# Three groups of transposes and an earlier-planned carry in a 16-batch attention-and-mixing block

## The chip, the cores and the metric

The kernel runs on one core of a Trainium2 chip. The metric is the device time of one execution in microseconds; the median of several runs is compared. A profile is one further execution, with a record of every instruction of the five engines: PE (matrix products; its weight loads are shown as PEld), DVE (vector), ACT (scalar), POOL (general purpose) and SP, which here only issues DMA transfers.

## What is computed

The input x has 16 batches of 512 rows and 512 columns, ctx 16 batches of 512 rows and 1024 columns. Per batch, cut to what matters:

```python
h  = layernorm(x)                                  # rows
h  = rmsnorm(h, g_res) @ W_in.T + b_in             # "a" product
u  = rmsnorm(ctx, g_init)[:, :512] * const
s  = scan(s[t] = a * s[t-1] + u[t])                # over the 512 rows
x1 = x + h + s[plug]                               # gather of rows
y  = layernorm(x1);  yp = y shifted down by one row
k  = square(relu((mu_k*y + (1-mu_k)*yp) @ W_k.T))  # "k" product
r  = sigmoid((mu_r*y + (1-mu_r)*yp) @ W_r.T)       # "r" product
out = x1 + r * (k @ W_v.T)                         # "v" product
```

The rows plug come from running sums of an integer mask.

## The kernel before

**Tiling.** A batch's 512 rows lie on 128 partitions, four rows to each (j = 0 to 3). Each product of 512 x 512 by 512 x 512 is made of four output tiles of 128 x 512, and each tile of three passes of four matmuls: both operands are split into a high part that was rounded to fp32r and the rest, and high by high, high by low and low by high are added (`QW`, `gemm` at line 880). A tile's sum stands in one PSUM slot of the pool "ps". There are four such slots (`SLOTS`, line 308), and four of "tr" for transposes. In the trace the tiles are called pa, pk, pr and pw for the a, k, r and v products, their operands xh (x), m (mixed y) and ka (k after its square), each with the weights wh and wl.

**The chain of one batch.** ctx comes into cx tiles (five slots, four used by a batch). ACT squares them with a row sum (`sq`, line 707), POOL takes the power, DVE scales cx and runs the scan over the four rows of a partition (`scan_u`). What is carried from partition to partition is one more product, the carry pc (`scan`, line 744; from batch 2 on `carry3`, three matmuls of the high and low parts ch and cl). DVE adds pc to the four cx tiles, and SP writes them to a scratch tensor dr in DRAM (`put`, line 775). x comes in by a DMA; its statistics (`stat1`, line 654) go before b_in is added by a DMA that accumulates (`add_b`, line 696). Rows of dr are then gathered into x by four indirect DMAs on POOL that add (`gather`, line 816); from batch 4 on they come ahead of the a product's end (`NLATE`, line 438). `a_end` (line 809) is the DVE operation that adds pa, scaled, to x and so frees the PSUM slot. `norm2` (line 823) takes the statistics of x1 on DVE and makes y on ACT. `transp` (line 848) turns y, four 128 x 128 transposes on PE for each j, into the four tr tiles, and `mix` (line 860) makes m of them for k and for r: ACT writes pv, DVE adds to it, ACT rounds to the high part, and DVE or POOL takes the low part. Behind a k product ACT applies relu and the square and rounds (`k_mm`, line 904); behind r, ACT the sigmoid (sg); behind v, DVE multiplies by sg and DVE or POOL adds to x, which SP stores.

**What sets the order.** Every such step is a piece, given to a planner by `add`. The first loop over batches gives each PE piece a due time (lines 1078 to 1090): in period i come the a product of batch i+1, the k product of batch i, and then the tiles r0, r1, v0, r2, v1, r3, v2, v3 of batch i, numbered k = 0 to 7. `TAT` and, for named periods, `TAT_OF` (lines 320 and 321) say behind which k which transposes j of batch i+1 stand. `deadlines` (line 90) computes each piece's latest start backward from what needs it, where the piece's own length (`span`, line 58) includes its lead, and once more from the number of slots: who needs a slot that a later piece takes must be done before that. `order` (line 119) then runs through the engines and takes for each the ready piece with the earliest latest start, if its slots are free; it hands out the lowest free slot number. The program is written in this order, and each engine works its queue in that order, waiting at an instruction whose inputs or slot are not ready. SP's loads also wait for the PE piece that the plan has some time ahead of them (line 1272).

So a changed lead or due time can move any piece on any engine, and which slot a tile is given.

```python
lead=LEAD if b > 1 else 0.0          # of the carry, lines 750 and 767; LEAD = 12.0, line 441
return self.lead + s + (...)         # span, line 60
for jj in TAT_OF.get(i, TAT).get(k, ()):
    slot(("t", i + 1, jj), 0.43)     # lines 1087 and 1088
```

Of the kernel before, what the change touches and what calls it, by code (L numbers as in the profile page):

```python
# [316 lines left out]
}  # L317
PASS = 0.935
PERIOD = lambda i: (("a", i + 1), ("k", i))
TAT = {0: (0, 1), 2: (2, 3)}  # L320
TAT_OF = {0: {0: (0, 1, 2, 3)}, 1: {0: (0, 1, 2, 3)}, 2: {0: (0, 1, 2, 3)}}
AHEAD = 20.0
EASE = 1.0
SKIP = 6.0
# [114 lines left out]
NWHOLE = 2  # L439
Y_DVE = (0, 1, 2, 3)  # L440
LEAD = 12.0
HI_DVE = False
U_DVE = True
LOADS = ["raw2"]
# [7 lines left out]
def block_kernel(  # L452
# [59 lines left out]
    def add(engines, fn, r=(), w=(), new=None, **kw):  # L512
        if isinstance(engines[0], str):
            engines = (engines,)
        kinds = {}
        for n, v in (new or {}).items():
            kinds[n], spec[n] = v[0], v[1:]
        kw["stage"] = stage
        if engines is LO and ONLY.get(stage) is not None:
            kw["port"] = (DVE, POOL)  # L520
            engines = (LO[ONLY[stage]],)
        elif engines is HI:
            kw["port"] = (DVE,) if HI_DVE else ()
        elif engines is LO:
            kw["port"] = (DVE, POOL)
        elif engines[0][0] == POOL and "moves" not in kw:
            kw["port"] = (POOL,)
        plan.add(engines, fn, r, w, kinds, **kw)

    def K(name, *parts):  # L530
        return [(name, p) for p in (parts or (0,))]
# [4 lines left out]
    PS = (("ps",), [P, D], F32)  # L536
    PST = (("ps", "tr"), [P, D], F32)
    TRP = (("tr", "ps"), [P, D], F32)
    TR = (("tr",), [P, D], F32)
    HI = ((ACT, 0.52), (DVE, 0.34)) if HI_DVE else ((ACT, 0.52),)  # L540
    LO = ((DVE, 0.61), (POOL, 1.26))
# [202 lines left out]
    def scan(b):  # L744
        def carry(e):
            e.matmul(S[f"pc{b}"], scan_m, S[f"cx{b}_{NJ - 1}"][:, :D], start=True, stop=True)

        if b < NWHOLE:
            add((PE, 1.12), carry, K(f"cx{b}_{NJ - 1}") + K("consts"), K(f"pc{b}"),
                new={f"pc{b}": PST if b == 0 else PS}, lead=LEAD if b > 1 else 0.0)  # L750
        else:
            last, hi, lo = f"cx{b}_{NJ - 1}", f"ch{b}", f"cl{b}"
            TMPR = (("tmp",), [P, D], F32R)
            if b == NWHOLE:
                add((ACT, 0.3), lambda e: e.copy(scan_hi, scan_m), K("consts"), K("scan_r", 0))
                add((DVE, 0.2), lambda e: e.tensor_tensor(scan_lo, scan_m, scan_hi.bitcast(F32), ALU.subtract),
                    K("consts") + K("scan_r", 0), K("scan_r", 1))
            add((ACT, 0.52), lambda e: e.copy(S[hi], S[last][:, :D]), K(last), K(hi), new={hi: TMPR})
            add(LO, lambda e: e.tensor_tensor(S[lo], S[last][:, :D], S[hi].bitcast(F32), ALU.subtract),
                K(last) + K(hi), K(lo), new={lo: TMPR})  # L760

            def carry3(e):
                for i, (w, m) in enumerate(((0, hi), (0, lo), (1, hi))):
                    e.matmul(S[f"pc{b}"], (scan_hi, scan_lo)[w], S[m], start=(i == 0), stop=(i == 2))

            add((PE, 0.72), carry3, K(hi) + K(lo) + K("scan_r", 0, 1), K(f"pc{b}"),
                new={f"pc{b}": PS}, lead=LEAD if b > 1 else 0.0)
        for j in J:
            n = f"cx{b}_{j}"
            add((DVE, 0.6),  # L770
                lambda e, n=n, j=j: e.scalar_tensor_tensor(
                    S[n][:, :D], S[f"pc{b}"], ADEC ** (j + 1), S[n][:, :D], ALU.mult, ALU.add),
                K(f"pc{b}"), K(n))

            def put(e, n=n, j=j):
                if f"dr{b}" not in S:
                    S[f"dr{b}"] = dpool.tile([T, D], F32, tag="dr", name=f"dr{b}")
                e.dma_start(S[f"dr{b}"].rearrange("(p j) d -> p j d", j=NJ)[:, j], S[n][:, :D])

            add((SP, 0.5), put, K(n), K(f"dr{b}", j), moves=0.73)  # L780
# [288 lines left out]
    def slot(key, cost=3 * PASS):  # L1069
        nonlocal t  # L1070
        due[key] = t
        t += cost
# [5 lines left out]
    for i in range(NB):  # L1078
# [5 lines left out]
        for k, (w, j) in enumerate((("r", 0), ("r", 1), ("v", 0), ("r", 2), ("v", 1), ("r", 3), ("v", 2), ("v", 3))):  # L1084
            slot((w, i, j))
            if n1:
                for jj in TAT_OF.get(i, TAT).get(k, ()):
                    slot(("t", i + 1, jj), 0.43)
# [62 lines left out]
    def prepare_batch(b):  # L1151
# [34 lines left out]
        for j in J:  # L1186
            scan_u(b, j, one_go=b == 0 or U_DVE)
        scan(b)
        stage = ("stat1", b)
        for j in J:  # L1190
# [141 lines left out]
```

## Time and profile before

| | |
|---|---|
| median of 3 runs | 815.05 us (812.93 to 817.34) |
| profiled execution | 813.32 us, of which 811.2 us is the span from first to last instruction |
| granted clock of PE in it | 0.997 |
| matmul of a pass, 128 x 512, mean of a row | 396 to 400 ns; starts 0.233 us apart |
| DVE, a_end (x from pa) | 744 ns |
| DVE, carry added to cx | 684 ns |
| ACT, relu of pk / square of cx | 596 / 1061 ns |
| POOL, issue of one gather | 1715 ns |
| gathers waited for on the chain that ended last | 5.8% of the span |

PE's matmuls overlap: a row says 0.4 us, but the next one starts 0.233 us after it, so four of them, one pass, take 0.933 us. Engine time is best read from the distance of two starts. A stage of one batch is found on PE's list by its first pr matmul. Where a line ends in brackets, the engine was idle for the time in them, and the name in them is what ended the idle time.

### The profile page before, as it was taken

What the parts mean: (1) busy time and instruction counts of PE and PEld (TensorE: products, weight loads), DVE (VectorE), ACT (ScalarE), POOL (GpSimd) and SP (SyncE); (2) the same over time, 40 slices, a digit from 0 to 9 for tenths busy, and PEclk for the clock granted to TensorE, in tenths of its full rate; (3) what the DMA queues carried; (4) which work ended last, traced back from release to release, by engine and by line L of the source; (5) the groups of instructions that cost most, each with busy time, mean ns of one, the idle gap of its engine ahead of it and who ended that gap; (6) DMA issues with size and microseconds to landing.
All of it is one profiled execution on the core that took longest, in us unless ns stands there. A gap on an engine that the chain in (4) does not pass through costs nothing.

```text
span 811.2 us, 11218 instructions
## 1 busy us (share of the span) xinstructions
PE 789.8 (97%) x3627; PEld 624.8 (77%) x3627; DVE 616.2 (76%) x1323; ACT 486.7 (60%) x950; POOL 449.8 (55%) x374
## 2 busy tenths in 40 slices
PE   7998999999999999999999999999999999999997
PEld 4776777877777887878787887888778787888885
DVE  6899799989789497686968779685876869784622
ACT  5937496555484566757455775646666564655640
POOL 2843676464675465763647566565665647571300
PEclk9999999999999999999999999999999999999999
DMA  9857486884784773847668392866559477350001
GB/s 321 271 96 263 101 235 175 280 216 131 157 232 131 181 232 74 241 166 198 156 140 242 74 268 107 218 198 184 135 130 246 136 173 216 66 141 2 27 27 52
DMA packets 52554, 134.69 MB, mean 166 GB/s; under 512 B 4752, under 2 KB 5264, under 8 KB 50576
## 3 DMA queue, kind: packets, MB, share of 16 engines
q1 hardware_dynamic: 35744, 102.39, 36.9%
q0 software_dynamic: 16608, 31.46, 23.0%
q8 instruction: 28, 0.46, 0.2%
q14 instruction: 30, 0.25, 0.1%
q10 hardware_dynamic: 144, 0.13, 0.0%
HBM read 85.73 MB, written 33.55 MB: 147 GB/s over the span
## 4 chain that ended last, share of the span: by engine, by line
PE 62%; DVE 12%; DMA 9%; POOL 6%; issue 5%; ACT 4%; SPq 0%; POOLq 0%; DVEq 0%; ACTq 0%
PE pk L300 19%; PE pr L300 15%; PE pw L300 14%; PE pa L300 11%; DMA x<-dr,plug 6%; DVE cx L300 4%; PE tr L300 3%; DVE pv L300 2%; DVE x L300 2%; POOL m L300 2%; DMA dr<-cx 2%; POOL x L300 2%; ACT pv L300 2%; PE pc L300 1%; ACT junk L300 1%
## 5 line engine op out<-in xcount | busy, mean ns | idle before, releaser
L300 POOL TENSOR_TENSOR m<-pv,m 128x512 fp32r<-128x512 f32 x79 | 117.1, 1492 | 54.6 <-ACT m L300 23.3
L300 PE MATMUL pr<-whr,m 128*128 128x512 f32 x512 | 141.7, 400 | 0.8 <-ACT sg L300 0.8
L300 PE MATMUL pa<-wha,xh 128*128 128x512 f32 x512 | 136.0, 400 | 5.6 <-DVE x L300 2.7
L300 POOL DMA_INDIRECT x<-dr,plug x64 | 109.8, 1715 | 55.8 <-DMA dr<-cx 16.8
L300 PE MATMUL pw<-whv,ka 128*128 128x512 f32 x512 | 138.9, 397 | 0.6 <-ACT sg L300 0.6
L300 PE MATMUL pk<-m,whk 128*128 128x512 f32 x512 | 134.4, 397 | 2.5 <-DVE x L300 2.1
L300 ACT ACTIVATE pv<-tr,om 128x384 f32<-128x384 f32 (+1 forms) x256 | 100.5, 488 | 57.7 <-PE tr L300 44.6
L300 PEld LDWEIGHTS pa<-wha,xh 128*128 128x128 f32 x512 | 94.8, 188 | 33.4 <-DVE x L300 7.3
L300 PEld LDWEIGHTS pk<-m,whk 128*128 128x128 f32 x512 | 95.2, 188 | 27.9 <-DVE x L300 2.9
L300 PEld LDWEIGHTS pw<-whv,ka 128*128 128x128 f32 x512 | 95.6, 188 | 24.1 <-ACT sg L300 1.8
L300 PEld LDWEIGHTS pr<-whr,m 128*128 128x128 f32 x512 | 94.0, 188 | 22.3 <-ACT sg L300 1.2
L300 DVE SCALAR_TENSOR_TENSOR pv<-tr,small,pv 128x511 f32<-128x511 f32 x128 | 95.0, 743 | 11.3 <-ACT pv L300 9.2
L300 ACT ACTIVATE y<-x,r 128x512 f32<-128x512 f32 x48 | 39.0, 816 | 97.3 <-DVE r L300 95.3
L300 DVE TENSOR_TENSOR sg<-pw,sg 128x512 f32<-128x512 f32 (+1 forms) x65 | 44.0, 678 | 55.6 <-PE pw L300 55.4
L300 POOL TENSOR_TENSOR xh<-raw,xh 128x512 fp32r<-128x512 f32 x48 | 64.4, 1348 | 39.1 <-ACT xh L300 22.6
L300 POOL TENSOR_TENSOR x<-x,sg 128x512 f32<-128x512 f32 x14 | 19.3, 1378 | 113.9 <-DVE sg L300 94.5
L300 ACT CAST m<-pv 128x512 fp32r<-128x512 f32 x128 | 73.2, 628 | 15.1 <-DVE pv L300 12.2
L300 ACT ACTIVATE junk<-cx 128x1024 bf16<-128x1024 f32 x64 | 67.9, 1061 | 12.3 <-DMA cx<-cx 11.6
L300 ACT ACTIVATE sg<-pr 128x512 f32<-128x512 f32 x64 | 38.1, 598 | 56.5 <-PE pr L300 47.3
L300 PE MATMUL pa<-wla,xh 128*128 128x512 f32 x256 | 70.4, 398 | 0.3 <-POOL wla L300 0.3
L300 PE MATMUL pw<-wlv,ka 128*128 128x512 f32 x256 | 70.7, 398 | 0.0
L300 PE MATMUL pr<-wlr,m 128*128 128x512 f32 x256 | 70.3, 396 | 0.0
(116 smaller groups left out, 1300.7 us busy)
## 6 DMA issues: line engine op xcount, KB each, us to landing
cx<-cx SPq DMA_DIRECT2D x64, 512.0 KB, 6.2
dr<-cx SPq DMA_DIRECT2D x64, 256.0 KB, 3.4
out<-x SPq DMA_DIRECT2D x31, 512.0 KB, 2.8
x<-x SPq DMA_DIRECT2D x15, 1024.0 KB, 4.9
x<-bc POOLq DMA_DIRECT2D x14, 1024.0 KB, 8.1
raw<-xT SPq DMA_DIRECT2D x26, 512.0 KB, 7.5
wsa<-winT SPq DMA_DIRECT2D x2, 512.0 KB, 4.4
x<-x SPq DMA_DIRECT2D x4, 256.0 KB, 7.0
```

Of the source, the lines that this page charges most:

```text
L300: r = self._tc.keep_in_program_order(op(*args, **kwargs))
```

## The change

In the general table the sixteen transposes of the next batch no longer stand in two groups of eight, behind r0 and v0, but in three: those of j = 0 behind r0 (four), j = 1 and 2 behind r1 (eight) and j = 3 behind r2 (four). Periods 3 and 4 are put into the table of exceptions with the groups they had, so the new grouping holds from period 5 on, which is the seventh batch's transposes (batch 6, counted from 0). The lead of the carry's piece is 15 instead of 12 from batch 6 on.

```diff
-TAT = {0: (0, 1), 2: (2, 3)}
-TAT_OF = {0: {0: (0, 1, 2, 3)}, 1: {0: (0, 1, 2, 3)}, 2: {0: (0, 1, 2, 3)}}
+TAT = {0: (0,), 1: (1, 2), 3: (3,)}
+TAT_OF = {0: {0: (0, 1, 2, 3)}, 1: {0: (0, 1, 2, 3)}, 2: {0: (0, 1, 2, 3)}, 3: {0: (0, 1), 2: (2, 3)}, 4: {0: (0, 1), 2: (2, 3)}}
...
 LEAD = 12.0
+LEAD_LATE = 15.0
+NLEAD = 6
...
             add((PE, 1.12), carry, K(f"cx{b}_{NJ - 1}") + K("consts"), K(f"pc{b}"),
-                new={f"pc{b}": PST if b == 0 else PS}, lead=LEAD if b > 1 else 0.0)
+                new={f"pc{b}": PST if b == 0 else PS}, lead=(LEAD if b < NLEAD else LEAD_LATE) if b > 1 else 0.0)
...
             add((PE, 0.72), carry3, K(hi) + K(lo) + K("scan_r", 0, 1), K(f"pc{b}"),
-                new={f"pc{b}": PS}, lead=LEAD if b > 1 else 0.0)
+                new={f"pc{b}": PS}, lead=(LEAD if b < NLEAD else LEAD_LATE) if b > 1 else 0.0)
```

No instruction is added or removed. In the order that the planner makes of it, PE's queue of one later period changes like this (batch numbers from 0, T for four transposes of one j, C for a carry, three passes to a product):

```
before   pa9_0  pa9_1  pa9_2  pa9_3   pk8_0 to pk8_3
         pr8_0  T9_0 T9_1  pr8_1 (C10 behind its first pass)  pw8_0  T9_2 T9_3  pr8_2  pw8_1  pr8_3  pw8_2  pw8_3
after    pa9_0  pa9_1 (C10 behind its first pass)  pa9_2  pa9_3   pk8_0 to pk8_3
         pr8_0  T9_0  pr8_1  T9_1 T9_2  pw8_0  pr8_2  T9_3  pw8_1  pr8_3  pw8_2  pw8_3
```

The queues of DVE, ACT, POOL and SP move with it: the four gathers of a batch, for instance, stand together in POOL's queue of the new kernel, where they stood between the low parts of m.

## The prediction

> **What bounds the kernel now.** I read the busy shares first, then PE's waits, then PE in order of time, then one 48 us period on every engine. PE leads by far.
>
> ```profile
> PE 789.8 (97%) x3627; PEld 624.8 (77%) x3627; DVE 616.2 (76%) x1323; ACT 486.7 (60%) x950; POOL 449.8 (55%) x374
> ```
>
> PE does the same products in every batch, so a batch has a floor, and what a batch takes above it is waiting. The stages below run from one batch's first receptance product (pr) to the next one's.
>
> ```profile
> 460.00:508.40 48.40, 48.05 (x213) 38.16 (x212) 37.82 (x76) 29.97 (x57) 30.11 (x25) 1.00 0.62 174
> 556.70:605.30 48.60, 47.63 (x226) 38.00 (x226) 36.62 (x84) 30.55 (x57) 28.66 (x24) 1.00 0.58 153
> 653.00:701.30 48.30, 47.97 (x212) 37.95 (x211) 37.91 (x76) 29.99 (x57) 30.07 (x25) 1.00 0.61 164
> 701.30:748.60 47.30, 47.30 (x213) 38.24 (x212) 29.62 (x55) 23.57 (x44) 19.68 (x17) 1.00 0.40 89
> ```
>
> The first figures are the stage's length, then PE busy. The last stage has no wait: 47.3 us is the floor, at full clock. Six earlier stages, from 412.4 to 701.3, took 288.9, which is 5.1 above six floors; 0.5 of it is the plug counts in the stage of 556.7. So about 4.6 us of waiting there, and no more is to be had.
>
> ```profile
> PE pa L300 <- DVE x L300: 2.7, 5, 2.0
> PE pk L300 <- DVE x L300: 2.1, 3, 1.0
> ```
>
> These are PE's two largest waits (total, times, longest). Both are for DVE adding a pa product to x, which frees the product's PSUM slot. Why is DVE late? The chain before one of them:
>
> ```profile
> 585.29 1.89 POOL m L300
> 587.34 8.40 DMA x<-dr,plug
> 596.65 8.66 PE pk L300 x36
> ```
>
> The last gather of rows into x left POOL at 587 behind POOL's subtraction for m, landed 8.4 us later, and PE waited 1.0 for the add behind it. In an ordinary period the gathers stand as late, with m between them:
>
> ```profile
> 666.52 1.70 POOL L300 DMA_INDIRECT x<-dr,plug  x1 [1.36 <-DMA dr<-cx]
> 675.26 1.54 POOL L300 DMA_INDIRECT x<-dr,plug  x1 [0.16 <-PE pw L300]
> 682.99 0.74 DVE L300 SCALAR_TENSOR_TENSOR x<-pa,rs,x 128x512 f32<-128x512 f32 x1
> ```
>
> The first add comes 6 us after the last gather's end. There the recurring waits of 0.17, some 0.35 with the slower restart, come from DVE alone, which has the next batch's scan in between.
>
> **The skill.** "Perfetto Trace Analysis", Identifying Performance Opportunities, says that a gap that repeats on the engine that should be saturated can mean too few buffers for the next tile. The trace agrees: the gap recurs each period at pa, before a product whose slot DVE has just freed. "GPSIMD Engine Reference", Key points, says that GpSimd shares its SBUF interfaces with VectorE and collides with instructions with two SBUF inputs. The trace agrees: DVE's x<-x,sg took 0.69 us beside an idle POOL and 2.14 beside POOL's m. "TensorE: Matmul & The Clock Gate", Part 4, gives about 275 ns for a transpose in a kernel; the row here says 273, but four of them cost far less end to end, as follows.
>
> **The change, part by part.** (1) *Three groups.* The number of transposes is the same. What does a group cost by itself?
>
> ```profile
> 183.59 0.60 PE L300 MATMUL tr<-consts,y 128*128 128x128 f32 x4
> 183.95 1.18 PE L300 MATMUL pw<-wlv,ka 128*128 128x512 f32 x4
> 655.60 1.04 PE L300 MATMUL tr<-consts,y 128*128 128x128 f32 x8
> 656.39 1.17 PE L300 MATMUL pr<-whr,m 128*128 128x512 f32 x4
> ```
>
> From start to next start, four take 0.36 and eight 0.79. The four matmuls behind them then take 1.01 (184.96 minus 183.95) and 1.00 instead of 0.93. So four cost 0.43, eight 0.86, and the third group costs 0.0; bounds are minus 0.1 and plus 0.1 a batch. In the changed order the groups stand after pr 0, pr 1 and pr 2: the last four fall one product, 2.8 us, later, and so does the mix for k that needs all sixteen. From there to the k product stand 24 passes of 0.933, 22.4 us (25.2 before); the mix's chain took 663.6 to about 675 here (ACT pv, DVE pv, ACT m, then DVE or POOL). Hidden, with about 10 us left.
>
> (2) *The carry.* The lead of 15 is no shift by 3 us. In PE's order of the changed kernel the carry of batch b stands inside the second pa product of batch b-1; before, it mostly stood inside the second pr product of batch b-2, which comes behind that pa stage and the k stage. It moves up past 8 passes of pa, 12 of pk and 4 of pr, 24 passes or 22.4 us, from batch 6 on (counted from 0). All of its train moves: four DVE adds of pc (2.48 us), four writes of dr on SP, the loads of the next cx on SP behind them, the squares on ACT, the power on POOL, the scan on DVE, and the four gathers. The gathers then stand on POOL at the start of pr, over 20 us before the first add of pa, instead of between the m's; four in a row are some 7.5 us of POOL (four issues of 1.5 to 1.9), and behind them wait an add of x and the first m of the next mix, whose product is 20 us away. On SP the four writes of dr come behind the load of the next x, which was issued 5.3 us after the pa stage began (683.17) and takes 4.9 to land (median): 10.2, before DVE's statistics need it at 12.3. The gathers of batches 8 and 12 stay late, because they wait for plug; but DVE's plug steps no longer stand behind a scan there, so I count their waits (0.6 at 402 and 1.1 at 594, restart included) as gone.
>
> What goes: the 4.6 above; 0.9 of the stage before it (0.6 at 402, 0.3 at transposes and carry); of the 2.8 from 200 to 365, the 0.5 at pa near 250. The 0.9 near 240 stands before the first moved instruction on PE, and the 1.2 at 318 (a slot freed by ACT) probably comes back at another product. I add 0.5 for half of it. Sum 6.5 us.
>
> What comes: the four carry adds now stand on DVE in the pa stage, the busiest for it. Take the last V product's end as 0 and go along DVE's new order with the durations of before: product by sg 0.2 to 0.9; add to x 0.98 (group mean), 1.9; three mixes at 0.79, 4.3; pa add 0.74, 5.0; statistics 1.03, 6.1; two carry adds, 7.3; a small one 0.13 and pa add, 8.2; two carry adds, 9.4; statistics and pa add, 11.2; statistics and a small one, 12.3; two statistics of the next x at 0.80, 13.9; last pa add, 14.7. PE needs that slot for the second k product, after 15 passes and the carry (0.76): 14.8. So it touches. It is 0 when all goes well and 1 us when an add is caught by POOL (2.14 instead of 0.98). I take 0.2.
>
> ACT then has three squares of cx (1.05 each) in the k stage, which it did elsewhere before. From its first read of a k product to the end of its fourth: three sets of relu, square, cast at 1.92, one y 0.72, one cast of xh 0.54, three squares 3.2, the last relu 0.6: 10.8 us. PE frees it 11.4 (nine k passes, three pr passes, 0.43 of transposes, less 0.2). But the first read starts late: y of row 2 stands ahead of it and waits for DVE's last pa add (14.7 plus 0.1), then 0.72 and 0.54 give 16.1, where the product is ready at 15.0. So 0.5 us too late, less the wait DVE caused already: 0.25, bounds 0 and 1.2. With 0.1 for the slow restart that is 0.55 in each of the six periods with this order (pa of batches 7, 9, 10, 11, 13, 14), 3.3 us, and 0.1 each in the two others. Sum 3.5.
>
> Net: 6.5 less 3.5, 3.0 us. Against the profiled execution (813.32, of which the span is 811.2 and 2.1 lies around it) that is 810.3; the median of the three runs is 1.7 above that execution, and from 815.05 it gives 812.0.
>
> **Rivals.**
> - *All waits go, none comes* (18%): DVE and ACT keep ahead. For it speaks that the chain on DVE just fits by the sum above. 815.05 less 6.5 is 808.5.
> - *Even exchange* (12%): the wait only changes its releaser, from DVE's late add after a gather to DVE's late add after the carry. For it: both kernels hand out PSUM slots by the lowest free number, two in turn, so the reader's lateness counts as before. 815.
> - *Slower* (20%): ACT in the k stage. Place: the reads of k products behind y of row 2 and the three squares. Each us by which the first read slips beyond the 16.1 goes straight into pr's slot, once a period. It decides from 1.1 us of wait a period on (6.5 over six); at 2 us, which two contended adds on DVE ahead of the last pa add would give, it is 12 less 6.5, some 6 us: 821. Against it: ACT is idle for 2 us around its k reads in the period shown (idle 1.0 before one k read, 0.8 and 1.9 around the first sg).
> - That the lead doesn't move the carry is excluded: PE's order shows it moved.
>
> **How the numbers follow.** Forecast 50%, 812.0, own range 809.5 to 814.5. Half a per cent, 4.1 us, is about what a measurement tells from no change: below 811.0 counts as faster. That takes the "all go" case and two fifths of mine, 0.38; same takes the rest of mine and most of the even exchange, 0.40; slower its own case and the slow end of the even exchange, 0.22. For 8 in 10 the range reaches from 807 to 820.
>
> **What would show it.** Right: gathers of ordinary batches at the start of pr with none waited for at pa; no PE wait at pa over 0.2; stages of 47.5 to 48.0; what waits remain stand at the second k product (for DVE x) and at pr 0 or 1 (for ACT kr). Transposes in groups of 4, 8 and 4 still at 0.43 per four. Wrong: ACT's k reads late by more than 1 us each period, POOL blocked by the four gathers in a row, or a carry on PE that waits for cl.

## The result, and the profile after

The changed kernel took 818.06 us (median of 20 runs, 816.40 to 820.70), the kernel before 813.85 (20 runs). The ratio is 1.0051, 95% interval 1.0041 to 1.0061: 4.2 us slower where 3 us faster was forecast. The profiled execution of the changed kernel took 819.69, its span 817.9. Its page has the same 3627 PE instructions as before:

```profile
PE 791.6 (97%) x3627; PEld 626.4 (77%) x3627; DVE 598.4 (73%) x1324; ACT 484.8 (59%) x950; POOL 450.2 (55%) x373
```

DVE is busy 18 us less than before: its adds x<-x,sg took 0.80 us on the mean instead of 0.98, its low parts of ka 0.72 instead of 0.92, and the planner exchanged 17 low parts of ka and 17 of m between DVE and POOL. The shorter times fit fewer collisions with POOL, which no run tests. By itself this is worth nothing: PE sets the time. Three stages, each from one batch's first pr product to the next one's (start and end, length, then busy us of PE, PEld, DVE, ACT and POOL, granted clock, busy share of the DMA engines, GB/s):

```profile
419.80:467.70 47.90, 47.61 (x213) 38.14 (x211) 34.74 (x77) 29.71 (x58) 27.43 (x22) 1.00 0.71 182
563.00:612.90 49.90, 48.89 (x230) 38.43 (x229) 38.93 (x87) 29.70 (x58) 27.48 (x23) 1.00 0.60 164
660.80:708.50 47.70, 47.39 (x212) 38.24 (x211) 34.18 (x76) 28.72 (x55) 29.00 (x23) 1.00 0.51 133
```

The six ordinary stages between the marks of batch 5 and 13 took 286.2 us in all, where they took 287.8 before (with one carry counted in each). But a stage with plug counts (the second line; there are two, from the first pr product of batch 6 and of batch 10) took 49.9, where the two took 48.0 and 48.6 before. PE's largest waits behind the first stages (total, times, longest) are others than before:

```profile
PE pr L300 <- ACT sg L300: 1.6, 1, 1.6
PE cp L300 <- ACT sg L300: 1.5, 2, 0.7
PE pr L300 <- ACT kr L300: 1.2, 4, 0.3
PE pk L300 <- ACT kr L300: 0.8, 3, 0.3
PE pc L300 <- POOL cl L300: 0.6, 1, 0.6
```

The four short waits of pa for DVE's x (0.17 or 0.18 us each) are gone. The fifth of that name, 2.0 us at 66 us, stands in the kernel's first stages in both kernels. The gathers stand at the start of pr, as forecast, and PE waits for none of them; here the stage began at 660.76:

```profile
665.37 1.70 POOL L300 DMA_INDIRECT x<-dr,plug  x1 [0.17 <-issue]
672.03 1.54 POOL L300 DMA_INDIRECT x<-dr,plug  x1 [0.30 <-issue]
```

In place of the old waits stand several kinds of wait for ACT. To see their weight I cut the time at two marks, the first pr product of batch 2 and of batch 5 (counted from 0), up to the first of batch 14. Between the marks the work is the same but for carry 7 (0.76 us, the difference of the 47.27 and 46.51 of stages with one carry and none), which I take out on both sides. What lies ahead of batch 2 is left out: that mark stood between 171.2 and 175.6 us in the profiles of all kernels, though the orders of PE, ACT, DVE and POOL are the same up to there.

| | passage: batch 2 to 5 | steady: batch 5 to 14 |
|---|---|---|
| before | 143.9 | 432.4 |
| after | 147.1 | 432.5 |

So from batch 5 on the change is an even exchange, and the loss, 3.2 us, lies where the carry passes from its old place to the new one. The medians differ by 4.2; the other 0.9 these two executions can't place. The passage on PE and ACT (start, us, engine, operation; idle time and what ended it in brackets):

```profile
271.96 1.10 PE L300 MATMUL pk<-m,whk 128*128 128x512 f32 x4
272.29 1.06 ACT L300 ACTIVATE junk<-cx 128x1024 bf16<-128x1024 f32 x1 [1.86 <-DMA cx<-cx]
...
273.35 0.80 ACT L300 ACTIVATE y<-x,r 128x512 f32<-128x512 f32 x1
274.05 0.57 ACT L300 ACTIVATE sg<-pr 128x512 f32<-128x512 f32 x1
...
274.68 1.19 PE L300 MATMUL pr<-whr,m 128*128 128x512 f32 x4 [1.62 <-ACT sg L300]
```

PE ends four matmuls at about 273 and begins the next product at 274.68, 1.62 us late, because its PSUM slot is freed by the sigmoid at 274.05. That sigmoid was not late for want of its input: ahead of it in ACT's queue stands a square of cx7, for which ACT was idle 1.86 us until its load landed. Here the k and r products of batch 4 alternate on PE, and ACT frees the slots of both. The second new place is the plug stage:

```profile
382.25 0.68 DVE L300 TENSOR_TENSOR sg<-pw,sg 128x512 f32<-128x512 f32 x1
...
383.01 1.29 POOL L300 TENSOR_TENSOR x<-x,sg 128x512 f32<-128x512 f32 x1 [8.91 <-DVE sg L300]
...
384.33 0.60 ACT L300 ACTIVATE sg<-pr 128x512 f32<-128x512 f32 x1 [7.28 <-POOL x L300]
...
384.97 0.54 PE L300 MATMUL cp<-ohj,oh 128*128 128x4 f16 x16 [0.74 <-ACT sg L300]
```

Read it upward. The plug counts on PE need the slot that the sigmoid of r tile 2 reads; that sigmoid needs a buffer that POOL's add of x frees; the add needs DVE's product by sg, and DVE had been busy with one-hots and the scan since 375. ACT had been idle for 7.28 us and POOL for 8.91. The third place, once in each of four ordinary stages:

```profile
469.71 1.06 ACT L300 ACTIVATE junk<-cx 128x1024 bf16<-128x1024 f32 x1
470.67 0.18 ACT L300 ACTIVATION_READ_ACCUMULATOR junk<-cx 128x1 f32 x1
470.76 0.57 ACT L300 ACTIVATE kr<-pk 128x512 f32<-128x512 f32 x1
```

```profile
470.50 0.60 PE L300 MATMUL tr<-consts,y 128*128 128x128 f32 x4
471.39 1.20 PE L300 MATMUL pr<-whr,m 128*128 128x512 f32 x4 [0.30 <-ACT kr L300]
```

Two squares of cx stand ahead of the last relu of k, and pr tile 1, which now has four transposes ahead of it instead of eight, comes 0.43 us earlier and finds its slot not yet read. With the slower restart that is 0.55 us.

### The profile page after: what moved, and what is told of

Read it like the earlier page. It is cut to its first block, busy times and chain, and to the rows that moved or that the text cites. A ratio compares the mean times of both kernels' runs of the same rounds, so it can differ in the third digit from the quotient of the medians.

```text
span 817.9 us, 11194 instructions
## 1 busy us (share of the span) xinstructions
PE 791.6 (97%) x3627; PEld 626.4 (77%) x3627; DVE 598.4 (73%) x1324; ACT 484.8 (59%) x950; POOL 450.2 (55%) x373
## 5 line engine op out<-in xcount | busy, mean ns | idle before, releaser
L300 POOL TENSOR_TENSOR m<-pv,m 128x512 fp32r<-128x512 f32 x96 | 134.4, 1415 | 109.3 <-ACT m L300 32.7
L300 POOL DMA_INDIRECT x<-dr,plug x64 | 111.8, 1746 | 45.5 <-issue 17.0
L300 DVE TENSOR_TENSOR ka<-kr,ka 128x512 fp32r<-128x512 f32 x52 | 37.6, 723 | 81.3 <-ACT ka L300 81.1
L300 ACT CAST m<-pv 128x512 fp32r<-128x512 f32 x128 | 76.6, 647 | 33.7 <-DVE pv L300 23.7
```

Source lines behind the costliest of these rows:

```text
L300: r = self._tc.keep_in_program_order(op(*args, **kwargs))
```

## The experiments

My first theory: the three groups are free, and both the passage and the plug stages come from the carry's move. The rival: the groups cost. Each part alone:

```diff
 e1:  changed kernel with
-LEAD_LATE = 15.0
+LEAD_LATE = 12.0
 e2:  changed kernel with
-TAT = {0: (0,), 1: (1, 2), 3: (3,)}
+TAT = {0: (0, 1), 2: (2, 3)}
```

> The three groups of transposes as in the changed kernel, the carry's lead left at 12 everywhere. Own theory (the groups cost nothing by themselves; the 4.2 us that the changed kernel is slower come from the carry being moved up: about 2 at the passage from the old place to the new one near 270 us, about 2 in the two periods with plugs): within 1 us of the kernel before, and no wait of PE for sg (pr4_0's PSUM slot) near 272 us. Rival (a switch between projection and transposes costs about 0.4 us each time): 3 to 4 us slower than the kernel before, spread evenly over the periods.

> The longer lead as in the changed kernel, the transposes in two groups of eight throughout. Own theory: about as slow as the changed kernel, 3 to 5 us over the kernel before, with the wait of about 1.6 us for sg near 272 us still there, since everything up to 290 us stands as in the changed kernel; in the two periods with plugs a wait of PE of 1 us or more. Rival (the groups are to blame): no slower than the kernel before, perhaps 1 to 3 us faster, as the waits of PE for the add of x in the first projection stage are gone.

My own theory's expectations both fell; of e2's rival, "no slower than the kernel before" held. e1 took 836.15 us (ratio 1.0255, 1.0236 to 1.0275), e2 814.41 (1.0002, 0.9987 to 1.0018). e2 still has the wait near 272 (2.15 us in its profile), so the passage belongs to the lead; but its steady part took 428.3, 4.1 less than before:

```profile
417.60:465.10 47.50, 47.46 (x211) 38.29 (x212) 33.64 (x75) 30.59 (x59) 31.86 (x26) 1.00 0.65 177
560.30:608.60 48.30, 48.01 (x229) 38.33 (x227) 38.34 (x87) 28.72 (x55) 26.54 (x22) 1.00 0.65 171
```

The longer lead does bring what was forecast of it, 4 us, and the three groups take 4.1 back: some 3 in the two plug stages (49.9 against 48.3 and 48.4), 1.8 in the four stages with a wait for kr, less 0.7 in the two stages ahead of the plug stages. e1 is the groups with a late carry. There the gather is late as in the kernel before, and worse:

```profile
409.73 0.75 DVE L300 SCALAR_TENSOR_TENSOR x<-pa,rs,x 128x512 f32<-128x512 f32 x1 [3.33 <-DMA x<-dr,plug]
```

```profile
410.54 1.81 PE L300 MATMUL pk<-m,whk 128*128 128x512 f32 x4 [1.78 <-DVE x L300]
```

and pr waits for ACT's sg six times, 6.9 us in all. Two windows of half clock (last section) add some 3 us. So the groups were no free addition: from batch 5 on, every wait of PE in e1 is for ACT or DVE.

Next, single moves within one engine's queue, all other orders and all buffer slots (the moved piece's own excepted) being those of the parent. e3 is for the passage, e4 for the plug stages:

```diff
 e3, ACT:
+    for j in (1, 2, 3):
+        behind = find(ACT, "ka4_2", "kr4_2") if j == 1 else find(ACT, "sq7", f"cx7_{j - 1}")
+        move(ACT, find(ACT, "sq7", f"cx7_{j}"), behind)
 e4, DVE:
+    for b in (6, 10):
+        move(DVE, find(DVE, f"pw{b}_0", f"sg{b}_0"), find(DVE, f"oh{b + 5}"))
```

> The changed kernel with three squares of batch 7 (cx7_1 to cx7_3) moved on ACT alone to behind the activation of sg4_0 and the cast kr4_2; every other order and every buffer slot is that of the changed kernel. Own theory (a square that waits for its load stands ahead of the activation that frees pr4_0's PSUM slot): 2.0 to 2.5 us faster than the changed kernel, 1.7 to 2.2 over the kernel before; the wait near 272 us goes from 1.6 us to under 0.4. Rival (PE loses there because carry 6 comes early and its clock or its operands are late anyway): no change beyond 0.5 us, another wait takes its place.

> The changed kernel with two products moved on DVE alone: sg6_0 and sg10_0 (times pw) directly behind the one-hots oh11 and oh15 instead of behind the remaining steps of the scan that follow; every other order and slot is that of the changed kernel. Own theory (scan steps and one-hots ahead of the product delay POOL's add of x, so the tmp slot, so ACT's sg_2, so the PSUM slot that the plug's counts need): 1.0 to 2.0 us faster than the changed kernel, and the two waits of PE for sg near 383 and 576 us go from 0.7 us to under 0.2. Rival (the one-hots, which stay ahead, already make the add late): under 0.5 us, the waits stay at 0.5 or more. Second rival: the scan steps, now later, make the carry or the first matmuls of the plug wait, and the time doesn't change.

e3: 817.04 (1.0043, 1.0026 to 1.0059); the wait near 272 went, one of 0.84 for the next batch's sg came at 293. e4: 816.86 (1.0033, 1.0023 to 1.0043); both waits of 0.7 went, the plug stages took 49.3 and 48.8. The directions held; e3's size did not (1.0 under the changed kernel where I had 2.0 to 2.5).

Is it the groups' place on PE or what the planner does on the other queues for their sake? e7 puts PE's transposes back into pairs, e9 puts those of e2 into three groups, nothing else; e6 has e3, e4 and the squares of batches 8 to 15 behind the last relu of k; e8 is e2 with the move of e3.

> The changed kernel with the transposes of batches 6 to 15 put back on PE alone into two groups of eight, at the places that they have in e2_lead_only; the orders of DVE, ACT, POOL and SP and all slots are the changed kernel's. Theory A (what costs in the three groups is their place on PE: two quarters of y are transposed 2.8 us later): the time falls to that of e2_lead_only, 3 to 4 us under the changed kernel. Theory B (what costs is the orders of DVE and ACT, which the planner makes anew for the groups: two squares of cx ahead of the last relu of k, scan steps ahead of the first product of a plug period): the plug periods stay as they are (wait of 0.7 for sg at each), and only the wait for kr behind the first four transposes is covered by the 0.43 us of four more: 1.5 to 2.5 us under the changed kernel.

> The mirror image: e2_lead_only with the transposes of batches 6 to 15 put on PE alone into three groups of four, eight and four at the places of the changed kernel; the orders of DVE, ACT, POOL and SP and all slots are those of e2_lead_only. Theory A (place on PE): 3 to 4 us slower than e2_lead_only, like the changed kernel. Theory B (the orders of the other queues): within 1 us of e2_lead_only, no wait of 0.7 for sg at the plugs and none of 0.3 for kr behind the first four transposes.

> The changed kernel with both moves of e3 and e4 and, for batches 8 to 15, the squares of cx quarters 2 and 3 on ACT behind the last relu, square and cast of the k stage instead of ahead of it. Theory B: e3 and e4 gave 1.0 and 1.2 us, the four waits of 0.3 for kr with their restarts (0.55 each) and the two of 0.2 (0.38) are another 3.0, so about 5 us under the changed kernel, 1 us under the kernel before; no wait for kr over 0.1. Rival: the squares, now 2.6 us later, make the scan on DVE late, and the product by sg or the gathers behind it wait instead: no more than 2 us under the changed kernel.

> The kernel with the lead alone and the move of e3 on ACT in addition (three squares of batch 7 behind the activation of sg4_0 and the cast kr4_2). Own theory: the wait of 2.15 us for sg near 271 goes, and, as in e3, about half of it comes back within 20 us: 1 us under e2_lead_only, so 0.7 us under the kernel before. If all of it stays gone: 2.5 us under e2_lead_only.

None of the four came as my theories had it (e6's rival, at most 2 us under the changed kernel, held in size): e7 818.91, e9 829.38, e6 818.61, e8 823.18 (ratios in the table). In e7 and e6 the waits for kr at pr 1 are gone and the four ordinary stages took 47.2 to 47.7, so this cost can be had back on either side, by eight transposes ahead of pr 1 or by the squares behind the relu. But the plug stages took 50.6 to 51.3 (three of these four hold a window of half clock, worth 1.5 to 1.6 us each; last section), and e8 lost at places where e2 had no wait. The reason for e8 is in POOL's queue:

```profile
621.23 1.70 POOL L311 DMA_INDIRECT x<-dr,plug  x1 [6.38 <-DMA cx<-cx]
```

The gather waits 6.4 us for a transfer and leaves 10 us into its stage, in e2 5 us. My edit had moved more than it said. These kernels plan twice, the second time with every queue's order and every slot given; but the program lets each SP load go behind a product on PE that the plan puts some time ahead of it, and in the second plan that product is another one, mostly an earlier one, for 67 to 83 of the loads. In this stage SP issued the loads of raw at 605.97, 5 us ahead of the first pr product; in e2 at 618.25, 10 us behind it. So these runs mix the move, the earlier loads and, in places, the half clock.

Before mending that, the passage itself, with the planner as it was. If it is one event with a price, it may be cheaper elsewhere (where e10's text says batch 3, the mark is that of batch 2):

```diff
 e10: two groups throughout       e11: two groups       e12: three groups
-NLEAD = 6                       -NLEAD = 6            -NLEAD = 6
+NLEAD = 8                       +NLEAD = 7            +NLEAD = 8
```

> Transposes in two groups of eight throughout, and the longer lead from the ninth batch on (NLEAD 8 instead of 6), so that carries 6 and 7 stay where the kernel before has them and the passage falls between carry 7 in the second pr product of batch 5 and carry 8 in the last pa product of batch 7. Theory (in the steady periods the longer lead with two groups is worth about 4 us; the passage from one place of the carry to the other took about 3 us back near 270 us, where three streams of products meet): the region from 170 to 315 us as in the kernel before (about 144 us from the first pr of batch 3 to that of batch 5), the periods behind it at 47.4 to 48.4 as in e2_lead_only: 3 to 4 us under the kernel before. Rival (every passage costs some 3 us wherever it is): equal to the kernel before, with the wait now near 365 us.

> As e10, with the longer lead from the eighth batch on (NLEAD 7): carry 6 stays as in the kernel before, carry 7 stands in the last pa product of batch 6. Theory: 2 to 4 us under the kernel before; the wait of 1.6 to 2.2 us for sg near 272 us is not there, since the loads of batch 7 are issued behind the stage in which k and r meet. Rival (a passage costs 3 us wherever it is): equal to the kernel before.

> The changed kernel with the longer lead from the ninth batch on (NLEAD 8): three groups of transposes as there, the passage as in e10. Theory (the passage and the groups add up): the passage's 3 us are gone, those of the groups stay: 1 to 3 us under the changed kernel, near the kernel before; waits of 0.7 for sg at the plugs and of 0.3 for kr as in the changed kernel. Rival (in three groups a late carry costs more than in two, as in e1_groups_only, where one period took 52 us): slower than the changed kernel, by the period that still has carry 7 in the k stage.

e10 818.03, e12 818.17, neither as the theory had it: the passage's loss moved and grew, into a stage of 52.3 and 52.4 behind the mark of batch 5 (47.3 and 47.5 in the changed kernel and e2; e10's stage holds one carry more, e12's a window of half clock). e11 took 812.12, ratio 0.9989 (0.9980 to 0.9998), a hair under the kernel before and not the 2 to 4 us expected; its passage cost 1.2 where e2's cost 3.0. So the passage was free at none of these places, and its price depends on what meets there. e13 has the plug move and, for the batches of the four other stages alone, the squares behind the relu:

> The changed kernel with the move of e4 on DVE (sg6_0 and sg10_0 behind the one-hots) and, for batches 10, 11, 14 and 15 alone, the move of e6 on ACT (squares of cx quarters 2 and 3 behind the last relu, square and cast of k). Theory (what the three groups cost behind 320 us is two places where an in-order queue holds back the read of a PSUM slot: DVE's in the plug periods, ACT's in the four others): the periods after a plug period fall from 47.9 and 48.0 to the 47.2 and 47.6 of e6, the plug periods stay at the 49.3 and 48.8 of e4, so 2.2 us under e4_product_first and some 3.4 under the changed kernel, about 814.7, where e2_lead_only stands. Rival (the waits hang together: squares moved later make the scan, and so the plug periods or the gathers, late again): 1 us or less under e4_product_first.

816.40 (1.0029, 1.0016 to 1.0042). Its steady part took 429.4, 3.0 less than the changed kernel's, of the 3.4 expected; its passage took 149.0, and the clock was 0.50 behind the wait for sg there, at 273.85.

Then the control that has the early loads alone (c0), and repeats (f) in which the order is planned once, the moves are made in it, and every load is let go where its parent lets it go:

> The changed kernel with every order on every engine and every slot as it is; only the product on PE behind which a load of SP is let go lies earlier for 67 of 114 loads, as in e3, e4, e6, e7 and e13. If the earlier loads cost nothing: 817.5 to 818.7 us, and those runs stand as read. If they cost (a load of raw ahead of one of cx makes the squares, the scan or a gather late): 1 to 5 us slower than the changed kernel, and by that much those runs have to be read as faster.

> The changed kernel with the transposes of batches 6 to 15 in two groups of eight on PE alone, at the places of e2_lead_only; orders of the other queues, slots and the release of each load as in the changed kernel. Place on PE: 3 to 4 us under the changed kernel. Queue orders: ordinary periods without the waits for kr (47.2 to 47.5), plug periods no shorter than 49.5, so about 2 us under the changed kernel or less.

> e2_lead_only with the transposes in three groups on PE alone, at the places of the changed kernel; all else, the release of each load too, as in e2_lead_only. Place on PE with ACT's queue left as it was: as in e9 the sigmoid of r tile 1 stands behind eight ACT operations that read the last transposes, and PE waits for it by 0.5 us or more in nearly every period: 6 us or more slower than e2_lead_only. If the 15 us of e9 came from the early loads: within 2 us of e2_lead_only.

> The changed kernel with the moves of e3 (squares of batch 7), e4 (product by sg in the plug periods) and e13 (squares of batches 10, 11, 14, 15 behind the last relu of k), the release of each load as in the changed kernel. If the waits named are the cost of the groups and half that of the passage: periods of 47.2 to 47.6 and 48.4 to 48.9 behind 320 us, 1 us less between 170 and 320 us, so 3.5 to 4.5 us under the changed kernel, level with the kernel before or a little under it. If others take their place: 2 us or less under the changed kernel.

c0's steady part took 432.5, as the changed kernel's, and its passage 1.3 less. But this profile is of the fastest of its six executions, and its median, 818.80 (1.0086, 1.0067 to 1.0104), is slower against the kernel before than the changed kernel's (1.0051). So that early loads cost nothing in that order is shown for the one execution only. f7 took 818.90, not some 2 us under the changed kernel as expected; its stages from batch 5 on are those of e7 to 0.1 us, and PE waits for DVE's sg and ACT's sg in both plug stages (0.74 and 0.80 in the first). Putting back PE's place alone brings next to nothing: 433.2 in the steady part, 1.5 of it half clock, against 432.5. f9 took 824.85, as expected for the place with ACT's queue left as it was: of e9's 13.7 us in the steady part, 4.4 came from the loads and 9.3 did not, most of that from this, in nearly every stage:

```profile
480.85 3.02 ACT L300 ACTIVATE pv<-tr,om 128x384 f32<-128x384 f32 x8 [5.98 <-PE tr L300]
483.71 0.65 ACT L300 ACTIVATE sg<-pr 128x512 f32<-128x512 f32 x1
```

```profile
484.41 0.97 PE L300 MATMUL pr<-whr,m 128*128 128x512 f32 x3 [0.48 <-ACT sg L300]
```

ACT's eight reads of transposes stand ahead of the sigmoid, and the last transposes now come 2.8 us later. Neither place on PE nor queue order alone is "the" cost: with PE's new place and the old queues the steady part takes 437.6 (f9), with the old place and the new queues 433.2 (f7), with both new 432.5.

f14 took 814.82. The waits at 272 and for kr at pr 1 are gone, but the plug stages took 50.4, not the 48.4 to 48.9 expected, with the product moved ahead and yet

```profile
378.61 1.27 POOL L300 TENSOR_TENSOR x<-x,sg 128x512 f32<-128x512 f32 x1 [9.46 <-DVE cx L300]
```

POOL's add waits for DVE's cx, the scan, which it does not read. The program lets some POOL operations, those marked as reading through the same port as DVE, wait for the last such DVE operation planned ahead of them; f14 had kept that pairing, while e4 had made it anew. The last two kernels:

```diff
 f15: f14 and
+    for b in (6, 10):
+        add = find(POOL, f"sg{b}_0", f"x{b}")
+        ...
+        turn[add.n] = find(DVE, f"pw{b}_0", f"sg{b}_0").n
```

> f14 with one thing more: POOL's adds of x behind sg6_0 and sg10_0 take their turn at the port behind the moved product and no longer behind the scan steps that now follow it. If the port rule was what held them: the add at once behind the product, no wait of PE for sg at the plugs over 0.2, plug periods of 48.4 to 49.0 instead of 50.4, so 2.5 to 3.5 us under f14. If the add, now beside DVE's scan, slows both: less than 1 us.

> e2_lead_only with the squares of batch 7 behind sg4_0 and kr4_2 on ACT, the release of each load as in e2_lead_only. If e8's loss came from the early loads: the waits of 3.3 us near 341 and 2.8 us near 630 are gone, periods as in e2_lead_only, 1 us less between 170 and 320 us: 0.5 to 1.5 us under e2_lead_only. If the later squares themselves make the scan of batch 7 late: the wait near 341 us stays.

```profile
377.28 0.69 DVE L300 TENSOR_TENSOR sg<-pw,sg 128x512 f32<-128x512 f32 x1 [0.45 <-PE pw L300]
...
378.06 1.67 POOL L300 TENSOR_TENSOR x<-x,sg 128x512 f32<-128x512 f32 x1 [6.87 <-DVE sg L300]
378.49 1.78 DVE L300 SCALAR_TENSOR_TENSOR cx<-cx,sq,bc 128x512 f32<-128x512 f32 x1
...
380.07 0.60 ACT L300 ACTIVATE sg<-pr 128x512 f32<-128x512 f32 x1 [5.92 <-PE pr L300]
```

In f15 the add follows its product at once; the DVE operation beside it takes 1.78 instead of 0.75 us, and no wait of PE follows from it. The sigmoid now waits for nothing but its own product, and the plug stages took 48.8 and 48.7. f15: 811.18 us, ratio 0.9976 (0.9968 to 0.9985). f8: 810.99, 0.9977 (0.9967 to 0.9986). Both are faster than both kernels, by about a quarter of a per cent against the kernel before, and f15 is the changed kernel with eleven squares, two products and two waits moved, and nothing else.

| kernel | groups, longer lead from batch | median us | ratio to before (95%) | passage | steady |
|---|---|---|---|---|---|
| before | two, none | 813.85 | 1 | 143.9 | 432.4 |
| after | three, 6 | 818.06 | 1.0051 (1.0041 to 1.0061) | 147.1 | 432.5 |
| e1 | three, none | 836.15 | 1.0255 (1.0236 to 1.0275) | 143.8 | 454.2 |
| e2 | two, 6 | 814.41 | 1.0002 (0.9987 to 1.0018) | 146.9 | 428.3 |
| e3 | three, 6 | 817.04 | 1.0043 (1.0026 to 1.0059) | 145.9 | 432.6 |
| e4 | three, 6 | 816.86 | 1.0033 (1.0023 to 1.0043) | 147.2 | 431.1 |
| e6 | three, 6 | 818.61 | 1.0059 (1.0042 to 1.0076) | 145.5 | 434.4 |
| e7 | two on PE alone, 6 | 818.91 | 1.0075 (1.0056 to 1.0094) | 146.5 | 433.1 |
| e8 | two, 6 | 823.18 | 1.0117 (1.0092 to 1.0143) | 145.7 | 438.2 |
| e9 | three on PE alone, 6 | 829.38 | 1.0217 (1.0177 to 1.0256) | 146.9 | 442.0 |
| e10 | two, 8 | 818.03 | 1.0056 (1.0043 to 1.0068) | 143.5 | 435.3 |
| e11 | two, 7 | 812.12 | 0.9989 (0.9980 to 0.9998) | 145.1 | 429.2 |
| e12 | three, 8 | 818.17 | 1.0057 (1.0044 to 1.0071) | 144.8 | 435.4 |
| e13 | three, 6 | 816.40 | 1.0029 (1.0016 to 1.0042) | 149.0 | 429.4 |
| c0 | three, 6 | 818.80 | 1.0086 (1.0067 to 1.0104) | 145.8 | 432.5 |
| f7 | two on PE alone, 6 | 818.90 | 1.0070 (1.0055 to 1.0085) | 148.8 | 433.2 |
| f9 | three on PE alone, 6 | 824.85 | 1.0137 (1.0120 to 1.0153) | 149.0 | 437.6 |
| f14 | three, 6 | 814.82 | 1.0026 (1.0014 to 1.0037) | 144.9 | 431.8 |
| f15 | three, 6 | 811.18 | 0.9976 (0.9968 to 0.9985) | 144.6 | 428.8 |
| f8 | two, 6 | 810.99 | 0.9977 (0.9967 to 0.9986) | 144.5 | 427.7 |

The two columns on the right are of one execution each, the medians of several, on several chips. In the nine kernels with the lead from batch 6 that leave the squares of batch 7 where the change puts them, the passage took 145.8 to 149.0; the three highest (e13, f7, f9) are those with half clock behind the wait for sg, which is worth 1.6, so without it 145.8 to 147.4. In the six with those squares moved it took 144.5 to 145.9.

## Why the prediction was wrong

- *Groups, switching.* Right: four transposes from 382.71 to the next start at 383.07 took 0.36 us, as four took before.
- *Groups, place.* Wrong: "the last four fall one product, 2.8 us, later ... Hidden, with about 10 us left". From batch 5 on no product of k waits for its mix. But I followed only the data from the transposes forward, and not what else queues with their readers. The groups, with the queue orders that the planner made for them, cost 4.1 us in the steady part (e2 against the changed kernel).
- *What goes in the steady part.* Right in kind: all four gathers early, no pa wait left. In size, e2 took 4.1 us less than before over the whole steady part, plug stages included, net of what came; I had 6.0 going there (the half of the wait at 318 included) and 3.5 coming, 2.5 net. One reading was loose: of the 2.7 us of pa's waits that I showed, 2.0 is the wait at 66 us, and what recurs later is four waits of 0.17 or 0.18 in three stages, not one each period.
- *What comes on ACT.* Right in cause: pr 1 waits for ACT's kr behind squares of cx. It came in four periods, those with the pa of batches 8, 9, 12 and 13: two of the six that I named, and the two that I had at 0.1. The price, 0.54 to 0.56 with the restart where I had 0.55, is met by luck, because 0.2 of mine was for DVE's last pa add at the second k product, a wait that did not come. And all four came only with three groups: my sum had 0.43 us of transposes ahead of pr 1, and 0.86 cover it; in e2 two waits for kr stand at pr 0 instead (0.42 and 0.34). I booked it to the carry.
- *Plug stages.* This step failed: "I count their waits (0.6 at 402 and 1.1 at 594, restart included) as gone" and "0.1 each in the two others", 1.5 us faster for the two. The waits did go, and PE's wait for the plug counts came instead: without carries the two stages took 98.3 against 96.6 before, 1.6 slower, a miss of 3.1 us. f15 shows how: with the product by sg ahead of the scan and POOL's add paired with it, the two stages take 2.2 us less; with the old pairing (f14) the wait stays, at 1.26.
- *The passage.* This step failed most: I read the waits from 200 to 365 us as things to be removed (0.5 at pa near 250, half of the 1.2 at 318) and never asked what the first early carry would meet. The wait at 318, behind the mark of batch 5, did go, and its stage took 1.2 less where I had 0.5. But up to that mark the change measured 3.2 us slower where I had 0.5 faster. With one carry counted in each stage, 2.4 of it is in the stage of batch 4 with the wait near 274, and 0.5 in that of batch 3, where the carry waits 0.57 for cl, one of the signs that I had named for being wrong. The moved train was known to me, squares on ACT included; I traced it in the steady stage alone. That squares ahead of their loads hold back ACT is shown by f14, f15 and f8 (no wait near 272, passage 2.2 to 2.6 us shorter than in the changed kernel or e2), though e3 with its early loads is no clear witness, since its control c0 was as fast there.

The two failed steps miss by 3.7 and 3.1 us; the rest of the steady part came out 0.5 better than my sum. That is 6.3 of the 7.2 between 3.0 faster and 4.2 slower; the other 0.9 lies outside the two stretches or between one execution and the medians. My rival "Slower" had the right sign and the right engine, ACT, but the wrong place: it put 2 us a period into the k stage.

Left open is why ACT's and DVE's plans differ between the two groupings in just this way (two squares ahead of the last relu, not one; the scan later against pw 0): it presumably comes from the planner's due times, which I did not take apart. What remains of the passage in f15, some 0.7 us, lies mostly in the stage of batch 3, where the wait of 0.57 for cl stands near 260, as it does (0.42 to 0.61) in all kernels with the early carry 6; no run moves it.

## What to carry to other kernels

When an operation moves in one queue, list for each other queue what now stands ahead of an operation that frees a PSUM slot or a buffer; an operation that waits for a load, put ahead of such an operation, hands its wait to PE. Check it in the steady stage, in each stage that differs from it (here the plug stages), and in the one where the old order passes into the new. Two parts of a change that look free apart must be tried apart: here, from batch 5 on, one was worth 4 us and the other took 4 back. And in an experiment that moves one instruction, see that waits derived from the order (release points of loads, turns at a shared port) are kept or moved on purpose.

## What the runs showed of the hardware

A short wait of PE can be followed by half speed. In e6:

```profile
385.33 0.54 PE L311 MATMUL cp<-ohj,oh 128*128 128x4 f16 x16 [1.74 <-ACT sg L311]
385.74 1.90 PE L311 MATMUL pw<-wlv,ka 128*128 128x512 f32 x4
387.43 1.91 PE L311 MATMUL pw<-whv,ka 128*128 128x512 f32 x4
```

Four matmuls take 1.7 us from start to start instead of 0.93, and the window from 387.40 to 389.10 shows a granted clock of 0.50. In f7's first plug stage the clock is 0.50 from 387.14 to 390.55, 3.41 us; its other plug stage has the same two waits ahead (0.74 or 0.75, then 0.80 or 0.79) and full clock. The same matmuls, from the plug counts to the next pr product, take 4.72 us in the one and 3.18 in the other, so the half clock costs 1.54.

The Trainium skill, "TensorE: Matmul & The Clock Gate", Part 1, has this half rate, entered after an idle window of about 3.4 us and left after a busy one as long. The trace agrees on the rate and on the length of the slow stretch. It does not agree that PE must idle so long: here waits of 0.80 us (f7, its second in 3 us) to 3.3 us (e12) came before it, and one of 2.15 us in e2 and one of 1.62 in the changed kernel did not bring it, so the length of a wait alone does not tell. Both plug stages of e6 and the first of e7 and of f7 owe 1.5 to 1.6 us to it, so a wait priced at its own length can be far too cheap.
